# The tail of a two-layer hybrid kernel: residuals loaded during the last matrix products, one room for all late frequencies, and a last piece in halves

## The chip, the cores and the metric

One core of a Trainium2 chip runs the whole program in one launch. The metric is the device time of one execution in microseconds. The core has TensorE (PE), with its weight loads shown apart as PEld, VectorE (DVE), ScalarE (ACT), GpSimd (POOL) and SyncE (SP); a "q" behind an engine's name is its sequencer, which issues transfers and waits. The transfers run on 16 DMA engines.

## What is computed

The input x is 8 sequences of 1024 tokens with 128 channels. Layer 0 is a convolutional attention, layer 1 a two-directional state space mixer and then a spectral filter bank. The last step of the reference, cut to what matters here:

```python
t = t + mixer(_ln_t(t), ...)
t = t + _L1_ffn_ref(_ln_t(t), sigma, phi, M_u, M_phi_plus, M_phi_minus, log_weights, gumbel)
...
def _compute_spectral(u, sigma, phi, Mpp, Mpm):
    U_plus, U_minus = _stu_conv(phi, u, PADDED_SL)      # causal convolution of u with 16 filters
    s = sigma ** SIGMA_POW
    out = jnp.einsum('btkd,k,kde->bte', U_plus, s, Mpp)
    out = out + jnp.einsum('btkd,k,kde->bte', U_minus, s, Mpm)
    return out
```

The kernel does the convolution in the frequency domain. For each of 128 frequencies it builds one 128x128 matrix out of all filters, applies it to the spectra of all sequences, and transforms back. What is added to the result is the residual: t after the mixer, with the direct taps already in it.

## The kernel before, in words

All of it is in `fast_kernel`; only its last two stages matter here.

**What lies in device memory ahead of them.** `ud` holds the spectra, `xa` (8 sequences x 128 x 2 blocks x 4 x 128 channels, float32) the residuals, `yd` (128 frequencies x 2 blocks x 8 sequences x 2 x 4 x 128) takes the filtered spectra.

**The matrix stage (lines 1484 to 1586).** The 128 frequencies go in 16 chunks of 8. For chunk c+1, `matrices` (L1499) makes matrices on PE from `mst` and `taps`; ACT and DVE copy them out of PSUM into `gs` (L1510, L1512), a tile of 64 KB per partition with two buffers. For chunk c, `apply` (L1533) multiplies them with the spectra `u` (two buffers), and `gather` (L1548 to L1554, ACT and DVE) adds the parts and stores them in `yd` with one transfer of SP (L1556), twice per chunk. The two are interleaved by hand; the loop runs from c = -1 to 15, so that in its last turn (c = 15) there is only `apply`. `fetch(c)` (L1564, SP) loads what chunk c gave for block 0 and sequences 0 to 3 back as rows of `early_yt`, two transfers of 64 KB each; it waits for that chunk's stores.

**The inverse stage (lines 1588 to 1631).** There are four pieces: two blocks k, two halves h of the sequences. A piece has its frequencies `yt` (two transfers of 1 MB each, L1599; the first piece uses `early_yt`), its residuals `res` (one transfer of 1 MB, L1601, three buffers) and four sums `z` on DVE (L1607). For each r of (0, 2, 1, 3) two matmuls of 128x128 by 128x512 (L1612; in float32 each is two instructions, so that a piece has 16) go into one PSUM tile, and DVE adds the result, times the selection `keep`, to the residual (L1619). ACT then issues the store of the piece (L1622, 1 MB). `yt` has two buffers, so the frequencies of piece 4 wait until piece 2 has been read, and the residuals of piece 4 wait until the store of piece 1 has left its buffer.

**What sets the order.** PE, DVE, ACT and POOL run the matrix stage in program order (`manual_schedule`). The order of SP's transfers is chosen by the scheduler. SP's queue is strictly in order: a transfer that waits keeps all later ones of SP waiting. Transfers of SP and ACT share eight semaphores in turn.

SP's order at the end of the kernel before: store of chunk 14 (second half), fetch 14 (first), store of chunk 15 (first half), fetch 14 (second), store of chunk 15 (second half), residuals of piece 1, fetch 15 (two), frequencies of piece 2 (two), residuals of piece 2, frequencies of piece 3 (two), residuals of piece 3, frequencies of piece 4 (two), residuals of piece 4.

Of the kernel before, what the change touches and what calls it, by code (L numbers as in the profile page):

```python
# [8 lines left out]
F32 = mybir.dt.float32  # L9
AF = mybir.ActivationFunctionType  # L10
ALU = mybir.AluOpType
AX = mybir.AxisListType
PSUM = bass.MemoryType.PSUM

P = 128
B = 8
T = 1024
NT = T // P
C = 128
# [11 lines left out]
NB = 2  # L31
# [14 lines left out]
def fast_kernel(ctx: ExitStack, tc: tile.TileContext, a: dict, out: bass.AP, bad: bass.AP):  # L46
    nc = tc.nc
# [12 lines left out]
    start = ctx.enter_context(ExitStack())  # L60
    starting = start.enter_context(tc.tile_pool(name="starting", bufs=1, side="right"))

    def ctile(shape, name):
        pool = passing
        if name in LASTING:
            pool = const
        elif name in ("fwd", "m_u"):
            pool = resid
        elif name in ("wqkv", "bout", "group", "row_le", "row_ge"):
            pool = starting  # L70
        return pool.tile(shape, F32, tag=name, name=name)

    xd = dram.tile([B, T, C], F32, name="xd")
    xa = dram.tile([B, P, NB, 4, C], F32, name="xa")
# [6 lines left out]
    yd = dram.tile([NF, NB, B, 2, 4, C], F32, name="yd")  # L81
# [23 lines left out]
    for d, m in enumerate((row_le, row_ge)):  # L105
        t = ctile([P, L], f"upto{d}")
# [11 lines left out]
        out=group, in_=group, pattern=[[-4, 32], [0, 4]], compare_op=ALU.is_ge, fill=0.0, base=0, channel_multiplier=1  # L118
    )
    nc.gpsimd.affine_select(  # L120
        out=group, in_=group, pattern=[[4, 32], [0, 4]], compare_op=ALU.is_ge, fill=0.0, base=3, channel_multiplier=-1
# [76 lines left out]
    keep = ctile([P, NB], "keep")  # L198

    fwd = ctile([P, 4, 2, NF], "fwd")  # L200
    inv = ctile([P, 4, 2, P], "inv")
# [385 lines left out]
    with ExitStack() as s:  # L587
# [6 lines left out]
        p2 = s.enter_context(tc.tile_pool(name="a_2", bufs=2))  # L594
        p4 = s.enter_context(tc.tile_pool(name="a_4", bufs=4))
        ps_t = s.enter_context(tc.tile_pool(name="a_ps_t", bufs=3, space=PSUM))
        ps_o = s.enter_context(tc.tile_pool(name="a_ps_o", bufs=1, space=PSUM))
# [172 lines left out]
        for n in range(len(units) + 2):  # L770
            if n < len(units):
                prs[n] = scores(*units[n])
            if 2 <= n and units[n - 2][2] % 2:
                b, half, j = units[n - 2]
# [3 lines left out]
            if 1 <= n < len(units) + 1:  # L778
                b, half, j = units[n - 1]
# [42 lines left out]
    with ExitStack() as s:  # L822
        p1 = s.enter_context(tc.tile_pool(name="b_1", bufs=1))
        p2 = s.enter_context(tc.tile_pool(name="b_2", bufs=2))
# [16 lines left out]
        def wide_psum(pool, name):  # L841

            return pool.tile([P, 1024], F32, tag="w", name=name)
# [419 lines left out]
        for at, u in enumerate(units[:-1]):  # L1263
# [41 lines left out]
            b = (u.b + 2) % B  # L1305
# [34 lines left out]
        u = units[-1]  # L1340
# [48 lines left out]
        po = wide_psum(ps_w, "pu0").rearrange("p (k r c) -> p k r c", k=NB, r=4)  # L1389
# [22 lines left out]

    with ExitStack() as s:
        mp = s.enter_context(tc.tile_pool(name="c_m", bufs=1, side="right"))
        mst = mp.tile([P, 32, C], F32, name="mst")
        early_yt = mp.tile([P, 2, 4, 4, C], F32, name="early_yt")

        with ExitStack() as s2:
            p1 = s2.enter_context(tc.tile_pool(name="f_1", bufs=1))
            p2 = s2.enter_context(tc.tile_pool(name="f_2", bufs=2))  # L1420
            ps_f = s2.enter_context(tc.tile_pool(name="f_ps_f", bufs=2, space=PSUM))
            ps_t = s2.enter_context(tc.tile_pool(name="f_ps_t", bufs=1, space=PSUM))
            ps_o = s2.enter_context(tc.tile_pool(name="f_ps_o", bufs=2, space=PSUM))
# [60 lines left out]
        with ExitStack() as s2:  # L1484
            p2 = s2.enter_context(tc.tile_pool(name="g_2", bufs=2))
            p3 = s2.enter_context(tc.tile_pool(name="g_3", bufs=3))
            ps_g = s2.enter_context(tc.tile_pool(name="g_ps_g", bufs=8, space=PSUM))
# [3 lines left out]
            def matrices(c, n, gs):  # L1491

                nonlocal turn
                pts = [ps_g.tile([P, 4, P], F32, tag="g", name=f"pg{c}_{n}_{g}") for g in range(4)]
                cols = slice(c * FC, (c + 1) * FC)
                for e in range(4):
                    for g in range(4):
                        rows = slice(g * 32, (g + 1) * 32)
                        nc.tensor.matmul(  # L1499
                            pts[g][:, e, :],  # L1500
                            lhsT=mst[rows, n * 4 + e, :],
                            rhs=taps[rows, cols].rearrange("p f q m i -> p (f q m i)"),
                            start=True,
                            stop=True,
                        )
                for g, pt in enumerate(pts):
                    to = gs[:, :, n * 16 + g * 4 : n * 16 + g * 4 + 4]
                    frm = pt.rearrange("p e n -> p n e")
                    if turn % 2:
                        nc.vector.tensor_copy(to, frm)  # L1510
                    else:
                        nc.scalar.copy(to, frm)  # L1512
                    turn += 1

            def loaded_spectra(c):

                u = p2.tile([P, 2, NB, B, 2, 4 * FC], F32, tag="u", name=f"u{c}")
                for k in range(NB):
                    nc.sync.dma_start(
                        u[:, 0, k].rearrange("p b i f -> p b (i f)"), ud[c][:, :, k].rearrange("p b i q f -> p b (i q f)")  # L1520
                    )
                nc.gpsimd.tensor_scalar(u[:, 1, :, :, 0, :], u[:, 0, :, :, 1, :], -1.0, None, ALU.mult)  # L1522
                nc.gpsimd.tensor_copy(u[:, 1, :, :, 1, :], u[:, 0, :, :, 0, :])
                return u
# [35 lines left out]
            def fetch(c):  # L1560

                rows = slice(c * FC, (c + 1) * FC)
                for i in range(2):
                    nc.sync.dma_start(early_yt[rows, i], yd[rows, 0, 0:4, i])  # L1564

            chunks = NF // FC
            gs, us, gathered = {}, {}, {}
            s2.enter_context(tc.manual_schedule(engines=IN_ORDER))
            for c in range(-1, chunks):
                if c + 1 < chunks:  # L1570
                    gs[c + 1] = p2.tile([P, P, C], F32, tag="gs", name=f"gs{c + 1}")
                    us[c + 1] = loaded_spectra(c + 1)

                for n in range(4):
                    if c + 1 < chunks:
                        matrices(c + 1, 2 * n, gs[c + 1])
                        matrices(c + 1, 2 * n + 1, gs[c + 1])
                    if c >= 0:
                        half, turn = divmod(n, 2)
                        py = ps_g.tile([P, 2, C], F32, tag="g", name=f"py{c}_{n}")  # L1580
                        apply(c, half, turn, gs[c], us[c], py)
                        apply(c, half, turn + 2, gs[c], us[c], py)
                        gather(c, half, turn, py)
                if c > 0:
                    fetch(c - 1)
            fetch(chunks - 1)

        with ExitStack() as s2:
            p2 = s2.enter_context(tc.tile_pool(name="i_2", bufs=2))
            p3 = s2.enter_context(tc.tile_pool(name="i_3", bufs=3))  # L1590
            ps_o = s2.enter_context(tc.tile_pool(name="i_ps_o", bufs=4, space=PSUM))

            def loaded(k, h):

                yt = early_yt
                if k or h:
                    yt = p2.tile([P, 2, 4, 4, C], F32, tag="yt", name=f"yt{k}_{h}")
                    for i in range(2):
                        nc.sync.dma_start(yt[:, i], yd[:, k, h * 4 : h * 4 + 4, i])  # L1599
                res = p3.tile([P, 4, 4, C], F32, tag="res", name=f"res{k}_{h}")  # L1600
                nc.sync.dma_start(res, xa[h * 4 : h * 4 + 4, :, NB - 1 - k].rearrange("b p r c -> p b (r c)"))  # L1601
                return yt, res

            def back(k, h, yt, res):
                z = p2.tile([P, 2, 2, 4, C], F32, tag="z", name=f"z{k}_{h}")
                for r, i, op in ((0, 0, ALU.subtract), (0, 1, ALU.add), (1, 0, ALU.add), (1, 1, ALU.subtract)):
                    nc.vector.tensor_tensor(z[:, r, i], yt[:, i, :, 2, :], yt[:, 1 - i, :, 3, :], op)  # L1607
                blk = NB - 1 - k
                for r in (0, 2, 1, 3):
                    po = ps_o.tile([P, 4, C], F32, tag="o", name=f"pz{k}_{h}_{r}")  # L1610
                    for i in range(2):
                        nc.tensor.matmul(  # L1612
                            po,
                            lhsT=inv[:, r, i, :],
                            rhs=z[:, r // 2, i] if r % 2 else yt[:, i, :, r // 2, :],
                            start=(i == 0),
                            stop=(i == 1),
                        )
                    nc.vector.scalar_tensor_tensor(  # L1619
                        res[:, :, r, :], po, keep[:, blk : blk + 1], res[:, :, r, :], ALU.mult, ALU.add  # L1620
                    )
                nc.scalar.dma_start(  # L1622
                    out[h * 4 : h * 4 + 4, blk * 512 : (blk + 1) * 512].rearrange("b (p r) c -> p b (r c)", r=4), res
                )

            pieces = [(k, h) for k in range(NB) for h in range(2)]
            got = [loaded(*piece) for piece in pieces[:3]]
            for n, piece in enumerate(pieces):
                back(*piece, *got[n])
                if n + 3 < len(pieces):  # L1630
                    got.append(loaded(*pieces[n + 3]))


@with_exitstack
# [803 lines left out]
```

## Time and profile before

| what | value |
|---|---|
| time, median of 3 runs | 1452.74 us (1451.16 to 1455.33) |
| the profiled execution's own time | 1452.17 us |
| its span | 1450.4 us |
| busy over the span: PE / PEld / DVE / ACT / POOL | 92% / 58% / 77% / 63% / 36% |
| last matmul of the matrix stage ends | 1399.9 us |
| first matmul of the inverse stage starts | 1409.47 us |
| last store is issued | 1443.24 us |
| transfers `yt` / `res` / `out` of the inverse stage | 6 / 4 / 4 of 1024 KB each |

Positions are microseconds from the start of the span. In the profile's rows, "L1612 PE MATMUL pz<-yt,inv" is the matmul of line 1612 that writes `pz` from `yt` and `inv`; "idle before <-X" is how long its engine had nothing to do, and what ended that. The chain of waits follows the end of the execution back through whatever released each step.

### The profile page before, as it was taken

To read this page: it belongs to the slowest core of one execution; us is meant where nothing else is said; L and a number is where in the kernel's file an instruction comes from. 1 tells how busy PE (TensorE), PEld (TensorE's weight loads), DVE (VectorE), ACT (ScalarE), POOL (GpSimd) and SP (SyncE) were. 2 spreads that over 40 slices of the span, in tenths; PEclk is the share of its full clock that TensorE was granted. 3 is DMA by queue.
4 is the path that set the end of the run, shared out by engine and by line. 5 is a ranking of instruction groups with operands and counts; after the bars stand their busy time and mean duration, and the time that the engine had idled before them with its cause. 6 is when DMAs were issued, how large, how long until landed. Compare 5 with 4: busy or idle time off the path is not lost. (4 is left out here: it accounts for less than half of the span.)

```text
span 1450.4 us, 45285 instructions
## 1 busy us (share of the span) xinstructions
PE 1341.4 (92%) x19782; PEld 842.2 (58%) x19782; DVE 1119.2 (77%) x2138; ACT 915.4 (63%) x1421; POOL 528.1 (36%) x510
## 2 busy tenths in 40 slices
PE   5999999999998899999989999999789899999977
PEld 2223333233333566666666666666679899999963
DVE  5779889688768598989898989898554677777745
ACT  2666666666756677778777777776344455555520
POOL 3327866875500332334342323233377111111100
PEclk9999999999999999999999999999989999999989
DMA  7101111110002333434333444442368323222258
GB/s 178 41 1 30 45 38 37 37 52 23 8 1 47 82 79 75 103 75 103 89 90 89 91 93 108 96 98 48 99 200 223 97 70 91 73 76 69 72 149 320
DMA packets 139382, 123.09 MB, mean 85 GB/s; under 512 B 44808, under 2 KB 118152, under 8 KB 135080
## 3 DMA queue, kind: packets, MB, share of 16 engines
q1 hardware_dynamic: 137064, 115.93, 31.1%
q10 hardware_dynamic: 2112, 4.19, 0.8%
q8 instruction: 157, 2.57, 0.7%
q14 instruction: 49, 0.40, 0.1%
HBM read 78.15 MB, written 34.08 MB: 77 GB/s over the span
## 5 line engine op out<-in xcount | busy, mean ns | idle before, releaser
L692 ACT ACTIVATE pr<-pt 128x1024 f32<-128x1024 f32 x256 | 248.1, 1021 | 117.2 <-PE pt L687 115.7
L717 DVE TENSOR_TENSOR two<-pr,pr 128x1024 f32<-128x1024 f32 x128 | 163.4, 1317 | 21.4 <-ACT pr L692 20.5
L1512 ACT COPY gs<-pg 128x512 f32<-128x512 f32 x256 | 132.7, 602 | 64.2 <-PE pg L1499 47.8
L1510 DVE COPY gs<-pg 128x512 f32<-128x512 f32 x256 | 158.7, 682 | 15.1 <-PE pg L1499 9.7
L687 PE MATMUL pt<-q,k 32*128 32x512 f32 x1024 | 160.1, 653 | 7.0 <-ACT pr L692 4.7
L1499 PE MATMUL pg<-taps,mst 32*128 32x128 f32 x4096 | 145.9, 282 | 4.7 <-ACT gs L1512 3.8
L1499 PEld LDWEIGHTS pg<-taps,mst 32*128 32x128 f32 x4096 | 134.1, 190 | 16.7 <-issue 11.4
L922 POOL TENSOR_TENSOR ec<-ec,ct 128x2048 f32<-128x2048 f32 x16 | 83.4, 5212 | 163.9 <-ACT cums L864 143.0
L708 PE MATMUL po<-pr,v 128*32 128x512 f32 x1024 | 141.7, 609 | 0.0
L1533 PE MATMUL py<-gs,u 128*32 128x128 f32 (+1 forms) x4096 | 128.2, 277 | 0.2 <-DVE gs L1510 0.2
L964 DVE SCALAR_TENSOR_TENSOR xs<-xp,cw,xs 128x1024 f32<-128x1024 f32 x96 | 121.8, 1282 | 3.5 <-issue 1.7
L986 PE MATMUL pb<-bxt,wbc 128*128 128x512 f32 x256 | 115.7, 605 | 8.6 <-ACT zs L977 6.0
L1533 PEld LDWEIGHTS py<-gs,u 128*32 128x32 f32 (+1 forms) x4096 | 112.2, 141 | 7.7 <-DVE gs L1510 0.4
L1522 POOL TENSOR_SCALAR u<-u 128x512 f32<-128x512 f32 x16 | 23.9, 1497 | 229.2 <-PE pg L1499 157.6
L687 PEld LDWEIGHTS pt<-q,k 32*128 32x128 f32 x1024 | 47.3, 186 | 86.2 <-issue 30.3
L1085 DVE SCALAR_TENSOR_TENSOR state<-state,dec,pst 128x64 f32<-128x64 f32 x448 | 87.4, 274 | 1.1
L986 PEld LDWEIGHTS pb<-bxt,wbc 128*128 128x128 f32 x256 | 47.7, 192 | 67.1 <-issue 54.9
L1133 PE MATMUL sy<-lm,xdt 64*64 64x64 f32 x2048 | 68.3, 224 | 17.5 <-DVE state L1085 10.5
L1194 POOL TENSOR_TENSOR rms<-rms_v,mhalf 128x8 f32<-128x8 f32 x16 | 26.2, 1636 | 151.3 <-DVE rms_v L1192 151.3
L708 PEld LDWEIGHTS po<-pr,v 128*32 128x32 f32 x1024 | 27.7, 110 | 89.5 <-issue 85.3
L1133 PEld LDWEIGHTS sy<-lm,xdt 64*64 64x64 f32 x2048 | 61.3, 136 | 30.8 <-issue 28.1
L908 POOL TENSOR_TENSOR lm<-cs,lm 128x2048 f32<-128x2048 f32 x16 | 57.9, 3617 | 46.6 <-DVE xs L964 19.5
(280 smaller groups left out, 2808.3 us busy)
## 6 DMA issues: line engine op xcount, KB each, us to landing
lm<-cd SPq DMA_DIRECT2D x32, 512.0 KB
ec<-cd SPq DMA_DIRECT2D x32, 512.0 KB
ud<-sp SPq DMA_DIRECT2D x8, 1024.0 KB
u<-ud SPq DMA_DIRECT2D x32, 256.0 KB
yd<-sums SPq DMA_DIRECT2D x32, 256.0 KB
moved<-state SPq DMA_DIRECT2D x48, 128.0 KB
yt<-yd SPq DMA_DIRECT2D x6, 1024.0 KB
X<-in_x SPq DMA_DIRECT2D x8, 512.0 KB
```

Source lines behind the costliest of these rows:

```text
L687: nc.tensor.matmul(pt[:, i, :], lhsT=k[rows, j * P : (j + 1) * P], rhs=q[rows, cols], start=True, stop=True)
L692: nc.scalar.activation(pr[:, 2 * g : 2 * g + 2, :].rearrange("p i t -> p (i t)"), pt.rearrange("p i t -> p (i t)"), AF.Exp, scale=SCALE,)
L708: nc.tensor.matmul(po[rows, :], lhsT=vs[b][:, j, rows], rhs=pr[:, h, :], start=(j == 0), stop=(j == NT - 1))
L717: nc.vector.tensor_tensor(two, sums["pr"][:, 2 * g : 2 * g + 2, :], pr[:, 2 * g : 2 * g + 2, :], ALU.add)
L964: u.convolved = nc.vector.scalar_tensor_tensor(acc, xp[:, at : at + T], cw[u.d][:, n, i : i + 1], acc, ALU.mult, ALU.add)
L986: nc.tensor.matmul(u.pb[:, i * 512 : (i + 1) * 512], lhsT=wbc[u.d][:, k, :], rhs=xt[:, at : at + 512], start=(k == 0), stop=(k == KC - 1),)
L1085: nc.vector.scalar_tensor_tensor(u.state[:, k, h, :], u.state[:, k - 1, h, :], u.dec[:, c, h, j : j + 1], u.pst[c][:, j, h, :], ALU.mult, ...
L1133: nc.tensor.matmul(u.py[c][h * HP : (h + 1) * HP, r, j, :], lhsT=left, rhs=right, start=(kind == 0), stop=(kind == 1 or k is None),)
L1499: nc.tensor.matmul(pts[g][:, e, :], lhsT=mst[rows, n * 4 + e, :], rhs=taps[rows, cols].rearrange("p f q m i -> p (f q m i)"), start=True, ...
L1510: nc.vector.tensor_copy(to, frm)
L1512: nc.scalar.copy(to, frm)
L1533: nc.tensor.matmul(py[t * 32 : t * 32 + 32 - 16 * m, q // 2, :], lhsT=u[:, i, m:, :, :, q * FC + f].rearrange("p k b i -> p (k b i)"), rhs ...
```

## The change

In the last turn of the matrix loop, where no further matrices are made, the free buffer of `gs` is taken as `room` (four slots of 16 KB per partition), and the room of `mst`, which nothing reads any more, as `res1`. Three of the four megabytes of residuals are loaded there: all of block 1 in one transfer of 2 MB (`res1`), and sequences 0 to 3 of block 0 in one of 1 MB (slot 0 of `room`). They stand in SP's queue ahead of the last stores and fetches. The frequencies of pieces 2, 3 and 4 go into slots 1, 2 and 3 of `room`, so that none waits for a buffer; the last residuals (1 MB) stand between those of piece 3 and piece 4. `z` uses the two buffers of `u`, and the PSUM tiles are the eight of the matrix stage instead of four of their own. The last piece is done in two halves of two sequences: 32 matmul instructions of 256 columns for 16 of 512, eight residual adds of half the size, two stores of 0.5 MB.

SP's order at the end of the changed kernel: store of chunk 14 (first half), residuals of block 1 (2 MB), store of chunk 14 (second half), residuals of block 0 (first megabyte), store of chunk 15 (first half), fetch 14 (first), store of chunk 15 (second half), fetch 14 (second), fetch 15 (two), frequencies of piece 2 (two), of piece 3 (two), last residuals, frequencies of piece 4 (two). On PE the four matmul instructions that use `early_yt` for one r now follow one another; before, the first factors of r = 0 and r = 2 came ahead of the second ones. Ahead of this tail the instructions of every engine stand in the same order in both kernels.

```diff
-        mst = mp.tile([P, 32, C], F32, name="mst")
+        mst = mp.tile([P, 32, C], F32, tag="mst", name="mst")
...
+            def load_residuals(k, b, n):
+                nc.sync.dma_start(
+                    res[k][:, b : b + n].rearrange("p b r c -> p b (r c)"),
+                    xa[b : b + n, :, k].rearrange("b p r c -> p b (r c)"),
+                )
+
...
                 if c + 1 < chunks:
                     gs[c + 1] = p2.tile([P, P, C], F32, tag="gs", name=f"gs{c + 1}")
                     us[c + 1] = loaded_spectra(c + 1)
+                else:
+
+                    room = p2.tile([P, P, C], F32, tag="gs", name="room")
+                    res = [room[:, :32, :], mp.tile([P, 32, C], F32, tag="mst", name="res1")]
+                    res = [t.rearrange("p (b r) c -> p b r c", b=B) for t in res]
+                    load_residuals(1, 0, B)
+                    load_residuals(0, 0, 4)
...
-        with ExitStack() as s2:
-            p2 = s2.enter_context(tc.tile_pool(name="i_2", bufs=2))
-            p3 = s2.enter_context(tc.tile_pool(name="i_3", bufs=3))
-            ps_o = s2.enter_context(tc.tile_pool(name="i_ps_o", bufs=4, space=PSUM))
...
+            pieces = [(k, h) for k in range(NB) for h in range(2)]
+            yts = [early_yt]
+            for n, (k, h) in enumerate(pieces[1:], 1):
+
+                yts.append(room[:, 32 * n : 32 * n + 32].rearrange("p (i b q) c -> p i b q c", i=2, b=4))
+                for i in range(2):
+                    nc.sync.dma_start(yts[n][:, i], yd[:, k, h * 4 : h * 4 + 4, i])
+                if n == 2:
+                    load_residuals(0, 4, 4)
+            for yt, (k, h) in zip(yts, pieces):
+                z = p2.tile([P, 2, 2, 4, C], F32, tag="u", name=f"z{k}_{h}")
...
+                size = 2 if (k, h) == pieces[-1] else 4
+                for b in range(0, 4, size):
+                    bs = slice(b, b + size)
+                    to = res[blk][:, h * 4 + b : h * 4 + b + size]
+                    for r in (0, 2, 1, 3):
+                        po = ps_g.tile([P, 4, C], F32, tag="g", name=f"pz{k}_{h}_{b}_{r}")[:, :size]
+                        for i in range(2):
+                            nc.tensor.matmul(
+                                po,
+                                lhsT=inv[:, r, i, :],
+                                rhs=z[:, r // 2, i, bs] if r % 2 else yt[:, i, bs, r // 2, :],
+                                start=(i == 0),
+                                stop=(i == 1),
+                            )
+                        nc.vector.scalar_tensor_tensor(
+                            to[:, :, r, :], po, keep[:, blk : blk + 1], to[:, :, r, :], ALU.mult, ALU.add
                         )
...
+                    nc.scalar.dma_start(
+                        out[h * 4 + b : h * 4 + b + size, blk * 512 : (blk + 1) * 512].rearrange(
+                            "b (p r) c -> p b (r c)", r=4
+                        ),
+                        to.rearrange("p b r c -> p b (r c)"),
                     )
```

More of the change, by code (lines that the diff above doesn't have):

```diff
@@ L1586, in fast_kernel @@
             fetch(chunks - 1)
-        with ExitStack() as s2:
-            p2 = s2.enter_context(tc.tile_pool(name="i_2", bufs=2))
-            p3 = s2.enter_context(tc.tile_pool(name="i_3", bufs=3))
-            ps_o = s2.enter_context(tc.tile_pool(name="i_ps_o", bufs=4, space=PSUM))
[L1593 to L1605, printed above, removed]
+            pieces = [(k, h) for k in range(NB) for h in range(2)]
[8 more added lines that the diff above has]
+                z = p2.tile([P, 2, 2, 4, C], F32, tag="u", name=f"z{k}_{h}")
                 for r, i, op in ((0, 0, ALU.subtract), (0, 1, ALU.add), (1, 0, ALU.add), (1, 1, ALU.subtract)):
@@ L1608, in back @@
                 blk = NB - 1 - k
[L1609 to L1617, printed above, removed]
-                        )
-                    nc.vector.scalar_tensor_tensor(
-                        res[:, :, r, :], po, keep[:, blk : blk + 1], res[:, :, r, :], ALU.mult, ALU.add
-                    )
@@ L1622, in back @@
[L1622 to L1631, printed above, removed]
+                size = 2 if (k, h) == pieces[-1] else 4
```

## The prediction

> **What bounds the tail now.** The change touches only the end, so I read the last 60 us: first the chain of waits, then busy time by stretches, then the instructions in order of time. In the chain (start, length, what) three transfers alternate with two stretches of work:
>
> ```profile
> 1401.63 7.35 DMA res<-xa
> 1408.98 0.49 issue
> 1409.47 9.94 PE pz L1612 x16
> ...
> 1420.34 9.47 DMA out<-res
> ...
> 1429.83 10.57 DMA res<-xa
> ...
> 1440.49 2.08 DVE res L1619 x3
> ```
>
> The first transfer is the residual load of piece 1. PE doesn't need it, but the fetch of `early_yt` was issued behind it. The last residuals are issued only when the store of piece 1 has landed (1420.34 + 9.47), and DVE's last sums wait for them until 1440.49. In the table by stretches (length; busy PE, PEld, DVE, ACT, POOL with counts; clock; DMA share; GB/s) two resources are full at once:
>
> ```profile
> 1391.00:1396.00 5.00, 5.00 (x186) 5.00 (x190) 2.80 (x9) 1.48 (x4) 0.00 (x0) 1.00 0.16 56
> 1396.00:1402.00 6.00, 3.89 (x144) 3.62 (x134) 2.26 (x10) 0.80 (x3) 0.00 (x0) 1.00 0.22 71
> 1403.00:1406.00 3.00, 0.00 (x0) 0.00 (x0) 0.00 (x0) 0.00 (x0) 0.00 (x0) 0.82 0.94 301
> 1406.00:1409.00 3.00, 0.00 (x0) 0.00 (x0) 0.00 (x0) 0.00 (x0) 0.00 (x0) 0.50 1.11 154
> 1412.00:1440.00 28.00, 26.25 (x58) 11.34 (x57) 16.87 (x26) 0.00 (x0) 0.00 (x0) 0.94 1.05 398
> ```
>
> From 1412 to 1440 transfers run at 398 GB/s, their limit here, and PE works 26.25 of 28 us. From 1391 to 1402, transfers are at 16 to 22%: room to which loads can move. Taking load off the DMA queue therefore wins only what PE waits: before piece 1, before piece 4, and at the end. In order of time:
>
> ```profile
> 1401.20 0.32 SPq L1556 DMA_DIRECT2D yd<-sums  x1
> 1401.63 0.37 SPq L1601 DMA_DIRECT2D res<-xa  x1
> 1403.52 0.64 SPq L1564 DMA_DIRECT2D early_yt<-yd  x2
> ...
> 1409.47 6.49 PE L1612 MATMUL pz<-early_yt,inv 128*128 128x512 f32 x8 [9.59 <-DMA res<-xa]
> ...
> 1436.60 1.98 PE L1612 MATMUL pz<-yt,inv 128*128 128x512 f32 x4 [1.75 <-DMA yt<-yd]
> ...
> 1440.49 2.73 DVE L1619 SCALAR_TENSOR_TENSOR res<-pz,keep,res 128x512 f32<-128x512 f32 x4 [1.31 <-DMA res<-xa]
> ...
> 1443.24 0.38 ACTq L1622 DMA_DIRECT2D out<-res  x1
> ```
>
> **The change, step by step** (all against the profiled execution, 1452.17 us, of which 1450.4 are its span).
>
> 1. Start of piece 1. The last store of `yd` is issued at 1401.20 and the fetch that needs it at 1403.52, 2.32 us later; the fetch lands at 1409.2 and 1409.9 (semaphore landings in the trace) because it stands behind the residuals issued at 1401.63. The same fetch for chunk 14, issued at 1396.36 into a quiet queue, had landed by 1399.0: 2.6 us. Early bound: 1403.5 + 2.6 + 0.3 from landing to matmul = 1406.4. But at 1406 to 1409 the queue moves only 154 GB/s, just when fetch and first frequencies read what was newly written; if that belongs to these reads and not to the residuals, only the time behind the residuals goes, some 1.7 us (their packets end at 1406.2 in the trace; the fetch's own would begin about 1 us after issue): 1409.5 - 1.7 = 1407.8. I take 1407.2, and 0.2 for stores behind the moved loads (step 5): 1407.4. Gain **2.1** (bounds 3.1 and 0).
>
> 2. PE's own work stays. Piece 1 takes 9.94 us (1409.47 to 1419.41), of which some 2.8 are the clock at 0.50 until 1415. PE will still idle 7.5 us (1399.9 to 1407.4) where it idled 9.6, and the clock fell 5 us after the last matmul (it is 0.82 over 1403 to 1406): I charge the same slow start. Pieces 2 to 4 take 6.86 us each (16 instructions, 0.43 apart).
>
> 3. Wait before piece 4. Piece 3 starts at 1426.10 and piece 4 at 1432.97, and PE would end at 1440.0; it ends at 1442.0. Gain **2.0**, if the frequencies of piece 4 land in time. They are needed at 1407.4 + 9.94 + 2 x 6.86 = 1431.1. Seven loads of 1.05 MB start near 1404.8: 2.8 us at 154 GB/s move 0.43 MB, the other 6.9 take 17.4 at 398: 1425.0; the stores of piece 1 and of a part of piece 2 go between (1.05 to 1.5 MB, 2.6 to 3.8 us), and a landing takes 1 to 1.6: 1428.6 to 1430.4. Just in time: I charge **0.3** (bounds 0 and 2). No load waits for a buffer any more; what is late next is this queue itself.
>
> 4. The end. Today the last add ends 1.2 us after the last matmul (1443.2 against 1442.0), since DVE waited for residuals. With them there, one half-size add is left: between 0.28 (128x128 add, L1553) and 0.75 (L1619), 0.4 by the middle. Gain **0.75**. The last store, issued at 1443.24, is followed by 7.2 us to the span's end; its packets fill 1444.1 to 1447.1. Half of these 3.0 us is 1.5; half of 1.05 MB at 398 GB/s is 1.3: gain **1.4** between the two. The 32 instructions of 256 columns aren't new to the trace: L539 has 128x256 in 3.62 us for 16, that is 0.216 apart and 6.9 for 32. Cost 0, because the weight load (0.19) still fits beneath; were it not to, 0.19 each on top would be 6, but the row excludes that.
>
> 5. The moved loads. `res1` waits for PE's last use of `mst` (1390.9); behind it in SP's queue stand the store of chunk 14 (ready 1394.2, so SP isn't late), the third megabyte, the stores of chunk 15 and the fetches. 3.15 MB at 398 GB/s are 7.9 us, from 1392 to 1400, and the two stores between them 1.3 us. Together, 3.67 MB at 398 take 9.2, to 1401.2, just when the last store is issued: cost about 0.2. At 301 GB/s (row 1403 to 1406) they take 12.2 us, to 1404.2, where the last store's packets ended at 1402.9 before: cost 1.3; at 154 it is the slower rival below. Below 0 nothing is to be had, since the store can't be issued before DVE is done. POOL's queue isn't passed. `z` in the buffers of `u` and eight PSUM tiles add no wait: both were last read at 1399.9, and pieces are four tiles apart. Issue order of PE in piece 1 costs nothing as long as both fetches land together (0.75 us apart today, charged in step 1's range).
>
> Sum: -2.1 - 2.0 + 0.3 - 0.75 - 1.4 = **-5.95**, 1446.2 on the profiled execution. The median of the runs shown is 0.6 above it: **1446.8**.
>
> [...]
>
> [...]
>
> **Rivals.**
> - *Piece 1 doesn't start earlier* (no change). The slow 3 us after 1406 come from reading fresh rows, and the store lands later behind the loads: step 1 gives 0, piece 4's frequencies come 1.5 late. Left are 2.0 - 1.5 + 0.75 + 1.4 = 2.65: 1449.5 by the profile, **1450.1** by the median. For it: 154 GB/s beside a PE that does nothing. Against: fetch 14 took 2.6 us on rows as fresh. Chance 0.22.
> - *The loads block the stores* (slower). `res1` and the third megabyte start from an idle queue and read at the 154 GB/s of 1406 to 1409: 3.67 MB take 23.8 us, from 1392 to 1416; the last store is done 13 us later than at 1402.9, and piece 1 starts not at 1407.2 but at 1420.2, 10.7 later than today: +10.7 - 2.0 - 0.75 - 1.4 = +6.6, 1458.7 by the profile, **1459.3** by the median. It is slower by over 0.3% once piece 1 starts 8.5 us late, that is from 20.8 us for the 3.67 MB, a mean below 176 GB/s. A delayed instruction fetch of PE behind these loads would add to it. For it: the row at 154. Against: that stretch lasts 3 us, and 28 us follow at 398. Chance 0.10.
> - *Frequencies get the whole queue and the clock rises sooner* (more gain): start at 1406.4, 1.4 us less of slow clock, nothing late: 5.95 + 1.0 + 1.4 + 0.3 = 8.65, **1444.1**. Chance 0.15, inside faster.
>
> **How the numbers follow.** A difference of 0.3% (4.4 us) is about what a measurement can tell from no change. The forecast has 0.53 and the better case 0.15: faster 0.68. Same 0.22, slower 0.10. The range reaches from the better case with 1 us more, 1443.0, over the no-change rival with 0.9 more, 1451.0.
>
> **What would show it.** Right: first matmul of the inverse stage at 1406.5 to 1408; no wait of PE ahead of piece 4; last store issued near 1438.7; transfers at over 300 GB/s in 1392 to 1401. Wrong: a first matmul after 1409.5 with the last `yd` store landing after 1405; PE idle between pieces on `yt`; `apply` of chunk 15 ending after 1400.5.

## The result, and the profile after

The changed kernel takes **1450.45 us** (median of 8 runs, 1447.21 to 1453.01), the kernel before in the same runs 1453.97 us (8 runs, 1449.04 to 1456.55): ratio **0.9975**, 95% interval 0.9958 to 0.9992. So it is faster, by about 3.5 us, not by the 5.95 us of the sum. By the prediction's own mark of 0.3% that size still counts as "no change", though the interval leaves out 1. Two repetitions below gave 0.9962 and 0.9973.

The profiled execution took 1450.32 us, its span 1448.4. To compare tails I count from **M**, the end of the last matrix matmul (L1499), because everything ahead of it is the same work: M is 1390.94 before and 1391.83 after, 0.9 apart in work that the change doesn't touch. Counted from M:

| us after M | before | after | difference |
|---|---|---|---|
| last `apply` matmul ends | 8.94 | 10.89 | **+1.95** |
| last store of `yd` issued | 10.26 | 12.19 | +1.93 |
| fetch 15 issued | 12.58 | 14.62 | +2.04 |
| first inverse matmul starts | 18.53 | 18.30 | -0.23 |
| last inverse matmul ends | 51.07 | 49.58 | -1.49 |
| last add ends | 52.27 | 50.11 | -2.16 |
| end of the span | 59.50 | 56.55 | **-2.95** |

The fetch does wait less (from its issue to the first matmul 3.67 us for 5.95), but everything ahead of it ends two microseconds later. The chain of waits of the changed kernel (start, length, what) shows why:

```profile
1391.83 8.27 PE py L1533 x231
1400.10 1.49 issue
1401.59 1.15 PE py L1533 x27
...
1404.02 2.42 DMA yd<-sums
...
1406.45 3.32 DMA early_yt<-yd
...
1410.12 31.30 PE pz L1624 x80
```

Two things are new. From 1410.12 to 1441.43 PE runs without a wait: the waits for `yt` and for the residuals are gone. And 1.49 us have appeared inside `apply`, which is nothing but matmuls whose data have long been there; "issue" means that the profile shows nothing that PE waited for. In order of time (start, length, engine, line, operation, count, idle time before it) the stop stands 28 matmuls before the end, and SP has two residual loads out by then:

```profile
1391.76 8.34 PE L1533 MATMUL py<-gs,u 128*32 128x128 f32 x292
1391.86 0.39 SPq L1567 DMA_DIRECT2D res<-xa  x1
...
1395.54 0.37 SPq L1567 DMA_DIRECT2D room<-xa  x1
...
1401.59 1.13 PE L1533 MATMUL py<-gs,u 128*32 128x128 f32 x28 [1.49 <-issue]
```

The kernel before does all 320 of these matmuls in one go:

```profile
1390.88 9.01 PE L1533 MATMUL py<-gs,u 128*32 128x128 f32 x320
```

What PE lacked were its own instructions, as experiments 1 to 4 show. Queue q8, of kind "instruction", brings them in packets of 16 KB (157 packets, 2.57 MB over the span of the kernel before, for PE's 39564 matmuls and weight loads: 252 a packet), and the profile counts these on the same 16 DMA engines. In the kernel before, the DMA view of 1395.9 to 1396.2 shows one such packet and no other queue (packets, MB, share of 16 engines); it starts 5.08 us after M:

```profile
q8 instruction: 1, 0.02, 19.4%
```

The same place in the changed kernel, counted from M, is 1396.9. There, over 1395.9 to 1399.2, the queue of the loads (q1) has all engines full and no instruction packet starts:

```profile
DMA packets 616, 1.24 MB, mean 375 GB/s; under 512 B 11, under 2 KB 11, under 8 KB 616
...
q1 hardware_dynamic: 616, 1.24, 103.3%
```

It comes in the next stretch, 1399.2 to 1399.5, 7.47 us after M, 2.4 us late:

```profile
q1 hardware_dynamic: 60, 0.11, 99.1%
q8 instruction: 1, 0.02, 19.7%
```

PE goes on 2.3 us after that packet starts. The table by stretches (length; busy PE, PEld, DVE, ACT, POOL; clock; DMA share; GB/s) answers to the one of before:

```profile
1391.80:1400.10 8.30, 8.30 (x293) 8.06 (x292) 4.26 (x15) 2.10 (x7) 0.00 (x0) 1.00 0.89 303
1400.00:1403.00 3.00, 1.23 (x30) 0.86 (x28) 0.00 (x0) 0.20 (x1) 0.00 (x0) 1.00 1.03 394
1406.00:1409.00 3.00, 0.00 (x0) 0.00 (x0) 0.00 (x0) 0.00 (x0) 0.00 (x0) 0.50 0.42 74
1411.00:1430.00 19.00, 19.00 (x40) 8.11 (x39) 12.69 (x20) 0.00 (x0) 0.00 (x0) 0.86 1.05 392
```

The empty room of 1391 to 1402 is filled as intended. From 1411 to 1430 PE is never idle (26.25 of 28 us before). The row of 1406 to 1409 can't be set beside the one of before (74 GB/s for 154), since fetch 15 is issued at 1406.45 here and at 1403.52 there. What can be compared are the 2 us in which the fetch and the first frequencies are read from `yd`, in the DMA view (packets, MB, share of 16 engines), 1407 to 1409 before and 1408 to 1410 after:

```profile
q1 hardware_dynamic: 92, 0.17, 105.2%
```

```profile
q1 hardware_dynamic: 128, 0.25, 94.7%
```

By share and count a packet takes some 0.37 us before and 0.24 after, where the loads of 1395.9 to 1399.2 take 0.09 a packet. These reads are slow in both kernels, and no residual load stands among them now.

### The profile page after: what moved, and what is told of

Its sections match the earlier page's. It is cut to its first block, busy times and chain, and to the rows that moved or that the text cites. A ratio compares the mean times of both kernels' runs of the same rounds, so it can differ in the third digit from the quotient of the medians.

```text
span 1448.4 us, 45312 instructions
## 1 busy us (share of the span) xinstructions
PE 1341.9 (93%) x19798; PEld 846.2 (58%) x19798; DVE 1118.5 (77%) x2142; ACT 915.1 (63%) x1421; POOL 528.0 (36%) x510
## 3 DMA queue, kind: packets, MB, share of 16 engines
q8 instruction: 157, 2.57, 0.8%
## 5 line engine op out<-in xcount | busy, mean ns | idle before, releaser
L1510 DVE COPY gs<-pg 128x512 f32<-128x512 f32 x256 | 158.7, 682 | 14.4 <-PE pg L1499 9.7
L1499 PE MATMUL pg<-taps,mst 32*128 32x128 f32 x4096 | 146.0, 281 | 4.0 <-ACT gs L1512 3.1
L1499 PEld LDWEIGHTS pg<-taps,mst 32*128 32x128 f32 x4096 | 134.0, 189 | 16.1 <-issue 11.5
```

Source lines behind the costliest of these rows:

```text
L1499: nc.tensor.matmul(pts[g][:, e, :], lhsT=mst[rows, n * 4 + e, :], rhs=taps[rows, cols].rearrange("p f q m i -> p (f q m i)"), start=True, ...
```

## The experiments

**Theory A**: the 2 MB load delays PE's instruction packet, PE stops, and that eats the gain of the earlier fetch. **Rival B**: the loads' writes or their use of memory slow `apply` itself, whatever the instruction packets do. **Rival C** (the first rival of the prediction): the fetch is slow because it reads fresh rows. All positions are counted from M of the same run.

**1. The loads alone, on the kernel before.** `idle` is read by nothing.

```diff
-        mst = mp.tile([P, 32, C], F32, name="mst")
+        mst = mp.tile([P, 32, C], F32, tag="mst", name="mst")
...
+                else:
+                    idle = mp.tile([P, 32, C], F32, tag="mst", name="idle")
+                    nc.sync.dma_start(
+                        idle.rearrange("p (b r) c -> p b (r c)", b=B), xa[:, :, 1].rearrange("b p r c -> p b (r c)")
+                    )
```

> The kernel before with one more transfer: 2 MB of residuals into the room of mst, at the place of the changed kernel's first moved load; nothing reads them, all else stays. Theory (instruction fetch of PE behind the load): a gap of PE of about 1.5 us, 8.3 us after the last matrix matmul, and the first matmul of the inverse stage about 2 us later than before (20.4 for 18.5). Rival (the gap is a dependency of the changed kernel): no gap, 18.5 as before.

Measured: 1454.39 us in one run. The direction is A's, the size is not: PE stopped once, for 2.90 us, 3.5 us sooner than expected, and `apply` ended at 15.21, 6.27 later than before. Its matmul groups, and PE's waits of 1380 to 1404 (us in total, times, longest):

```profile
1386.61 4.84 PE L1533 MATMUL py<-gs,u 128*32 128x128 f32 x164
1394.36 7.53 PE L1533 MATMUL py<-gs,u 128*32 128x128 f32 x156 [2.90 <-issue]
```

```profile
PE py L1533 <- issue: 2.9, 1, 2.9
```

The stop accounts for about half of the 6.27 us. The rest is PE's clock, which fell during the stop (table by stretches, ahead of the stop, with it, and behind it):

```profile
1386.70:1391.20 4.50, 4.50 (x164) 4.50 (x164) 2.79 (x9) 1.53 (x5) 0.00 (x0) 1.00 0.76 238
1391.20:1394.30 3.10, 0.25 (x8) 0.01 (x1) 0.06 (x1) 0.00 (x0) 0.00 (x0) 0.89 1.03 377
1396.00:1398.00 2.00, 2.00 (x44) 1.85 (x40) 0.89 (x4) 0.27 (x1) 0.00 (x0) 0.50 0.01 2
```

At a clock of 1.00 PE does 164 of these matmuls in 4.5 us, at 0.50 only 44 in 2 us.

The packet due at 1.0 (it starts 1.02 us after M in the kernel before) was served only at 5.09; the next ones at 8.79 and 14.4. In the changed kernel the packet due at 1.0 was served at 1.06, although the load there is issued at the same place (0.03 after M): it started at 1392.88, and the first packet of the load 0.04 us later, at 1392.92. So the first packet and the load's first packets run a race, and a lost one brings a stop 128 matmuls sooner: here a long one that cost the clock too, in experiments 2 and 8 the first of two.

**2. The same bytes without writing on-chip memory.** The load is a copy from device memory to device memory. A 64 KB store of `half`, put ahead, only sets its start.

```diff
+                if (c, n, turn) == (chunks - 2, 1, 0):
+                    nc.sync.dma_start(idle[:, 0, :C], half)
+                    nc.sync.dma_start(idle, xa[:, :, 1].rearrange("b p r c -> p b (r c)"))
...
+            idle = dram.tile([P, B, 4 * C], F32, name="idle")
```

> The kernel before with a copy of 2 MB inside device memory (plus 64 KB ahead of it to set its moment), at about the same moment; nothing reads it. It touches no on-chip memory but that first 64 KB. Theory (DMA engines busy, instruction fetch waits): PE stops for 1 to 4 us between 4 and 10 us after the last matrix matmul, with no packet of the instruction queue inside the copy. Rival (writing into on-chip memory slows PE's reads): no gap.

Measured: 1454.63 us in one run. Instruction packets at 3.85 and 8.44; PE stops after the same 164 and 292 matmuls:

```profile
1389.66 4.84 PE L1533 MATMUL py<-gs,u 128*32 128x128 f32 x164
1396.07 3.76 PE L1533 MATMUL py<-gs,u 128*32 128x128 f32 x128 [1.57 <-issue]
1400.37 1.13 PE L1533 MATMUL py<-gs,u 128*32 128x128 f32 x28 [0.54 <-issue]
```

`apply` ends at 11.77. Writes to on-chip memory are not needed for the stop, which takes that half of B away; the other half, memory reads, falls with the next run.

**3. The changed kernel with its instructions moved.** 32 matmuls near the beginning are done twice (the same result), so that packet boundaries move by 128 instructions, 64 matmuls with their weight loads; the loads stay.

```diff
-                for e in range(4):
+                for e in list(range(4)) * (2 if c == 0 and n < 2 else 1):
```

> The changed kernel with 32 matmuls of the very first matrices made twice (same result): 128 more PE instructions, 1200 us back into the stage's start, which moves the boundaries of 16 KB in PE's instruction stream about 2 us earlier against the program. Theory (the fetch that falls into the load waits until the load ends): the gap starts at about 6.4 instead of 8.3 us after the last matrix matmul and ends at the same 9.7, so it lasts about 3.4 us instead of 1.5; apply ends near 12.8 instead of 10.9. Rival (anything that depends on the place in the program or on the load alone): gap of 1.5 at 8.3, as in the changed kernel.

Measured: 1450.53 us in one run. The stop moved with the instructions, from after 292 matmuls to after 228, exactly 64 earlier:

```profile
1391.54 6.59 PE L1533 MATMUL py<-gs,u 128*32 128x128 f32 x228
1400.76 2.88 PE L1533 MATMUL py<-gs,u 128*32 128x128 f32 x92 [2.63 <-issue]
```

`apply` ended at 12.03. The stop was shorter than the 3.4 us expected, but its place is what B can't give: the traffic is the same, and the place of the stop follows the count of instructions.

**4. The moved loads put back into the tail**, one ahead of each piece's frequencies, all else as changed.

```diff
-                    load_residuals(1, 0, B)
-                    load_residuals(0, 0, 4)
...
             fetch(chunks - 1)
+            load_residuals(1, 0, 4)
...
-                if n == 2:
-                    load_residuals(0, 4, 4)
+                load_residuals(*((1, 4, 4), (0, 0, 4), (0, 4, 4))[n - 1])
```

> The changed kernel with its three moved megabytes of residuals back in the tail (piece 1's right behind the fetches of chunk 15, the others each behind the frequencies of the piece before); room, halves and eight PSUM tiles kept. Positions count from the end of the last matrix matmul (L1499). Theory (the loads keep PE's instruction fetch waiting): PE's apply of chunk 15 has no gap and ends at 9.0, as before, where the changed kernel has 10.9; the first matmul of the inverse stage comes at 15.6 to 16.6 (before 18.5, changed 18.3). Rival (the gap comes from the new buffers or from the order on PE): the gap of 1.5 us stays. On both the queue is the bound of the rest: PE waits 3 to 5 us for the frequencies of piece 4 and the residuals behind them end it within 1.5 us of the kernel before. Second question: if the fetch of early_yt lands within 2.9 us of its issue with a residual load behind it, slow reads come from the frequencies that follow it; if it needs over 3.3, from the fetch itself.

Measured: 1459.07 us in one run (1447.98 for one of before); M came 4.0 us later than in the changed kernel. `apply` ends at 8.93, without a stop, and the first inverse matmul starts at 15.73, 3.45 after its fetch was issued. So a residual load *behind* the fetch doesn't hold it up, and C falls as it was priced: piece 1 starts 3.45 us after the fetch's issue, against 5.95 before, although the rows are as fresh. A part of C stays. The fetch lands 3.36 us after its issue (3.32 in the changed kernel, by its chain), just over the mark of 3.3 that the expectation set for a fetch that is slow itself; chunk 14's took 2.6 us in the kernel before. Whether the age of the rows makes these reads slow, or their form (one fetch goes into 8 of the 128 partitions of `early_yt`), no run separates.

The 3 MB, however, now stand in the queue that the pieces wait for:

```profile
1430.78 2.84 PE L1624 MATMUL pz<-room,inv 128*128 128x512 f32 x6 [2.09 <-DMA room<-yd]
...
1439.50 0.70 PE L1624 MATMUL pz<-room,inv 128*128 128x256 f32 x2 [2.45 <-DMA room<-yd]
1442.27 2.93 PE L1624 MATMUL pz<-room,inv 128*128 128x256 f32 x6 [2.07 <-DMA room<-yd]
```

PE waits 6.6 us in three places, more than the 3 to 5 expected. The span ends at 61.35, 4.8 later than in the changed kernel and 1.85 later than before (at most 1.5 was expected). Moving the loads is right, in spite of the stop: 2.57 us of later start buy 8.42 us of a shorter inverse stage (1.05 of them are lost again between PE's last matmul and the end of the span).

**5. The last piece whole**, all else as changed.

```diff
-                size = 2 if (k, h) == pieces[-1] else 4
+                size = 4
```

> The changed kernel with its last piece whole again (16 matmuls of 512 columns, four adds, one store of 1 MB); all else stays. Positions from the last matrix matmul, or from the first matmul of the inverse stage where the start wanders. Forecast's view: the halves are worth 1.4 us behind the last add and 0.35 in the last add itself, and cost nothing on PE: from first matmul to span's end 38.3 + 1.7 = 40.0. Rival (halves give less, since the last piece's matmuls wait for z, 7.6 us instead of 6.9, and two stores queue behind each other): 38.3 + 0.5 = 38.8.

Measured: 1452.06 us in one run. From first matmul to the end of the span it takes 38.60 us, for 38.25 in the changed kernel, but that sum can't judge the halves: piece 1, which they don't touch, took 9.29 us here and 9.99 there, because the clock rose 4.7 us after its first matmul here and 6.1 there. From the first matmul of the last piece to the end of the span it is 15.58 us whole and 14.53 in halves (14.55 with the moved instructions, 14.20 and 14.57 in the repetitions). So halves win 1.0 to 1.4 us here, of which 0.36 is a wait of the whole piece for its frequencies; forecast were 1.7, by the rival 0.5. Behind the last matmul they save 1.23 us (8.19 for 6.96). They cost something on PE that the prediction set at nothing. In the changed kernel's last piece (order of time, the first half):

```profile
1433.85 1.89 PE L1624 MATMUL pz<-room,inv 128*128 128x256 f32 x8
...
1434.72 2.49 DVE L1614 TENSOR_TENSOR z<-room 128x512 f32<-128x512 f32 x4
...
1435.57 2.38 PE L1624 MATMUL pz<-z,inv 128*128 128x256 f32 x8
1436.06 0.30 PEld L1624 LDWEIGHTS pz<-z,inv 128*128 128x128 f32 x2 [0.29 <-DVE z L1614]
```

The matmuls that don't need `z` last 1.89 us in a half and 3.60 in a whole piece that waits for nothing; DVE first finishes the add of piece 3 and then needs 2.49 for `z`, so PE catches up with it.

**6. The loads spread.** One megabyte of block 1 is loaded at chunk 8 into a tile of its own, `early_res`; the other goes where the 2 MB went; the third waits until two quarters of chunk 15 are done. SP follows program order in the last turn.

```diff
+        early_res = mp.tile([P, 4, 4, C], F32, name="early_res")
...
-                    load_residuals(1, 0, B)
-                    load_residuals(0, 0, 4)
+                    load_residuals(1, 4, 4)
+                if c == 8:
+                    nc.sync.dma_start(
+                        early_res.rearrange("p b r c -> p b (r c)"), xa[0:4, :, 1].rearrange("b p r c -> p b (r c)")
+                    )
...
+                        if (c, n) == (chunks - 1, 1):
+                            load_residuals(0, 0, 4)
```

> The changed kernel with the moved loads spread: the residuals of piece 1 (1 MB) far earlier, in chunk 8, into 8 KB per partition of their own; those of piece 2 (1 MB) at the place of the 2 MB load, into mst's room; those of piece 3 (1 MB) behind the first store of chunk 15. SP's last transfers stand in program order. Theory: a load of 1 MB is through 4.6 us after the last matrix matmul, ahead of the fetch due at 5.1: no gap (if the fetch due at 1.0 isn't caught), apply ends at 9.0, first inverse matmul at 16.7 (changed: 18.3), span's end at 55 (changed 56.5, before 59.5): ratio to before 0.9965 to 0.997. Rival (bytes, not the length of one burst, slow PE): the gap stays over 1 us, end at 56.5, ratio 0.9975.

Measured (5 rounds): 1452.89 us, ratio 0.9985 (0.9969 to 1.0001). In the tail A holds: the packet due at 5.1 is served at 5.94, and PE stops for only 0.2 us (too short for the groups in order of time, which show 320 matmuls in one go); `apply` ends at 9.38.

```profile
1397.04 9.45 PE L1534 MATMUL py<-gs,u 128*32 128x128 f32 x320
```

But the third megabyte now stands before the last store: fetch 15 goes out at 15.05, piece 1 starts at 18.58, and PE waits 1.8 us before the last piece. The span ends at 56.22, 0.3 better than the changed kernel, where 55 was expected. In this execution (1455.21 us, above the median) M is at 1397.11, 5.3 us later than in the changed kernel; 4.6 of these are there already when the matrices of chunk 1 begin (1151.2 for 1146.6), ahead of the load in chunk 8. One trace can't say whether the worse median comes from there too.

**7. The same with the two tiles exchanged**, so that the third megabyte goes to the room of `mst` and the second to that of `gs`.

```diff
-                    res = [room[:, :32, :], mp.tile([P, 32, C], F32, tag="mst", name="res1")]
+                    res = [mp.tile([P, 32, C], F32, tag="mst", name="res0"), room[:, :32, :]]
```

> As e7, but the residuals of piece 2 go into the free buffer of gs, which is read until about 2.0 us after the last matrix matmul, so the load starts 2 us later and can't catch the fetch due at 1.0; those of piece 3 and 4 go into mst's room. Theory: the fetch due at 5.1 meets the last microsecond of that load and is late by up to 1.5 us, which PE's lead over its fetch (about 1.1) nearly hides: gap of 0 to 0.4, apply ends at 9.0 to 9.4, span's end at 55 to 55.5, and never the double stop of e2: ratio 0.9965 to 0.997, with less spread than e6. Rival: as for e7.

Measured (5 rounds): 1453.72 us, ratio 0.9982 (0.9962 to 1.0002); packet at 7.51, a stop of 1.4 us, `apply` to 10.83, a wait of 1.0 before the last piece, end at 56.36, M 1395.76. The expectation, a stop of at most 0.4 and an end by 55.5, missed: the packet due at 5.1 waited 2.4 us although the load ahead of it was half as large.

**8. Two bursts of a megabyte.** `early_res` as in 6; 1 MB right after the last matrices, the third behind the second store of chunk 14.

```diff
-                    load_residuals(1, 0, B)
                     load_residuals(0, 0, 4)
...
+                    if (c, n) == (chunks - 2, 3):
+                        res = [None, mp.tile([P, 32, C], F32, tag="mst", name="res1")]
+                        res[1] = res[1].rearrange("p (b r) c -> p b r c", b=B)
+                        load_residuals(1, 4, 4)
```

> As e7 (residuals of piece 1 in chunk 8, those of piece 2 at the place of the 2 MB load), but the residuals of piece 3 go behind the second store of chunk 14, so that their packets are gone before the last store, which they delayed in e7; SP in program order from chunk 14 on. Theory (a fetch waits for packets that already stand ahead of it, here at most one burst of 1 MB): the fetch due at 5.1 is served between 5.5 and 8, gap of PE 0 to 1.5 us, apply ends at 9.0 to 10.4; the last store is not held back (3.7 us from apply's end to the fetch of chunk 15, where e7 had 5.7), first inverse matmul at 16.6 to 17.8, span's end at 54.5 to 56 after the last matrix matmul (changed 56.6 and 56.8, e7 56.2). Rival (what the gap loses less the queue takes at piece 4): end at 56 or more, with a wait of over 1.5 us ahead of piece 4.

Measured (5 rounds): 1453.58 us, ratio 0.9986 (0.9965 to 1.0007). The profiled execution lost the race of experiment 1 with half the bytes: packets at 3.48 (due at 1.0) and 8.88, and two stops, again after 164 and 292 matmuls:

```profile
1393.12 4.83 PE L1534 MATMUL py<-gs,u 128*32 128x128 f32 x164
1399.20 3.75 PE L1534 MATMUL py<-gs,u 128*32 128x128 f32 x128 [1.26 <-issue]
1404.32 1.13 PE L1534 MATMUL py<-gs,u 128*32 128x128 f32 x28 [1.36 <-issue]
```

`apply` ends at 12.27 (10.4 at most was expected), the span at 57.34 (56). The rival's wait ahead of piece 4 isn't there either: PE has none in the inverse stage.

**9. The changed kernel again**, beside 5 to 7 and beside 8.

> The changed kernel once more, on the chip of the two that follow. Theory: the fetch due 1.0 us after the last matrix matmul races with the first packets of the 2 MB load (1.1). Where the fetch wins, as in the profile, PE stops once, for 1.5 us; where it loses, as with the idle load of e2, twice, for 6. So its times spread, and its mean gain over before is 1 to 4 us: ratio 0.997 to 1.000. Rival: the gap is always 1.5, ratio 0.9975 as measured.

> The changed kernel on the chip of e9, for a comparison of the two: one gap of 1.5 to 2.3 us in apply, the fetch of instructions served 7.5 to 8.1 us after the last matrix matmul, span's end at 56.5 to 57, ratio to before 0.996 to 0.9985. If e9 is better by its tail alone, it shows 1 to 2 us (0.1%) below this, about as much as the spread of the medians.

Measured (5 rounds each): 1450.35 us, ratio 0.9962 (0.9948 to 0.9977), and 1450.97 us, ratio 0.9973 (0.9951 to 0.9995). One stop in either profile, of 2.0 and 1.9 us, and the first packet at 1.07 and 0.90: none of the three profiles of the changed kernel lost the race. The "twice, for 6" of the first expectation took the 6 us of experiment 1 for two stops. None of the versions 6 to 8 beat it: their medians are higher, though the intervals overlap.

Taken together, the runs give the size of a stop. In those without moved instructions, PE reaches the matmul after the packet boundary 4.5 or 8.0 us after M when nothing held it before, and goes on 2.2 to 2.6 us after the packet's start. For the boundary at 8.0:

| run | packet starts | PE goes on | stop (start less 8.0) |
|---|---|---|---|
| loads spread (6) | 5.94 | 8.26 | 0.3 |
| changed | 7.47 | 9.76 | 1.8 |
| tiles exchanged (7) | 7.51 | 9.70 | 1.7 |
| changed, third time | 7.79 | 10.19 | 2.2 |
| last piece whole (5) | 7.85 | 10.30 | 2.3 |
| changed, again | 8.08 | 10.30 | 2.3 |

So the stop is the packet's start plus 2.3 less 8.0, and the packet of 5.1 may come about 0.6 us late at no cost. (The stops are the gap between the starts of two matmuls; the idle time that the trace gives is about 0.3 less, one matmul.) The clock can add to it. In the repetition beside 5 to 7 it falls after the stop:

```profile
1402.00:1402.70 0.70, 0.70 (x12) 0.20 (x4) 0.00 (x0) 0.00 (x0) 0.00 (x0) 0.50 0.44 149
```

There `apply` ends 1.6 us after PE goes on, in experiment 5 1.9, for 1.1 in the changed kernel.

## Why the prediction was right and wrong

It was right in sign, and the waits that it meant to shorten did get shorter; but the largest term, the earlier start, was nearly all eaten by a cost that the sum left out. The time lies inside the range near its slow end, 3.65 above the forecast. Counted from M, 3.0 of the 5.95 us are missing. Two of the prediction's own three signs of being wrong came true: `apply` ends at 1402.72 (after 1400.5), and the first matmul comes at 1410.12 (after 1409.5) with the last store of `yd` landing at 1406.44 (after 1405). M is 0.9 later here than in the profile of before; without that the matmul would come at 1409.2, but `apply` would still end at 1401.8. That the time is in the range all the same is partly luck. The slow end was set by the rival without a gain at the start, and a stop that this rival doesn't contain brought the total to within 0.4 of its 1450.1; a lost race as in experiments 1, 2 and 8 would have cost 1 to 4 us more. Step by step:

- **Step 5 is the one that failed.** "Cost about 0.2" counted only what stands behind the moved loads in SP's queue: the stores. That term was right: from the end of `apply` to the last store's issue 1.30 us for 1.32, and to fetch 15's issue 3.73 for 3.64. Instruction packets of PE, which go through the same engines from another queue, were mentioned only as an addition in a rival with 0.10, without a price. They cost **1.95**; that the stop comes from them is shown by experiments 1 to 4.
- **Step 1**: the fetch-to-matmul part was 3.67 us, as the prediction had it (3.7, from 1403.5 to 1407.2), a gain of 2.28. Gain of the start after step 5's loss: 0.23 for 2.1. The rival "piece 1 doesn't start earlier" has about the right total for the wrong reason: the store wasn't late behind the loads, it was issued late because `apply` ended late. Its doubt about the reads of fresh rows was half right: they are slow without the residuals too, but they took the fetch 3.3 us to its landing, not the 5.7 of before.
- **Step 2**: the clock stays low as charged (0.50 in the row from 1406). The idle time was 7.4 us for the 7.5 assumed. The clock rose 6.1 us after the first matmul where it had risen after 5.7, so piece 1 takes 9.99 us for 9.76 (to the first matmul of piece 2). Pieces 2 and 3 take 6.87 each, as the row had it.
- **Step 3**: the wait before piece 4 went, 2.0 us, and the 0.3 charged for the queue wasn't paid. It had little left: in experiment 6 the last frequencies are issued at 23.87 after M for 23.52 and needed 1.0 us sooner, since piece 1 is shorter, and PE waits 1.8 us.
- **Step 4**: the last add ends 0.52 us after the last matmul for 1.20, a gain of 0.68 for 0.75. The half-size store gains **0.79** for 1.4: 6.44 us from the last add to the end of the span, for 7.23. Most of its packets are out between 1442.5 and 1444.5, but single ones go on to 1446 and beyond. And "cost 0" of the halves was wrong: from its first matmul to the end of its last one the last piece takes 7.56 us, for 7.03 in pieces 2 and 3, since halves shorten the cover of `z`. The working excluded weight loads as a cost and didn't ask for DVE's `z`.

Sum from M: -0.23 at the start; on PE -2.01 for the wait, +0.53 for the halves and +0.23 for the clock in piece 1; -0.68 and -0.79 behind it: -2.95.

One sum in the slower rival is off, without effect here: a start 8.5 us late, reckoned back as its own 10.7 was, needs 21.7 us for the 3.67 MB, a mean of 169 GB/s, not 20.8 and 176.

What stays open: why M comes 4 to 5 us later than in the changed kernel in the profiles of experiments 4, 6 and 7 (1395.8 to 1397.1, for 1386.7 to 1393.2 in all others). Most of it (3.4 to 4.6 us) is there when the matrices of chunk 1 begin, ahead of every load that these edits move or add. Executions of one kernel differ by as much (the changed kernel's eight by 5.8 us), so it may be no more than that; a tail is judged here from M, not by the total of one execution. And how often the changed kernel loses the race for the first packet: three profiles can't tell.

## What to carry to other kernels

Before moving a large load into a stretch where the DMA engines look idle, look up the instruction queue in the DMA view: if an engine is running short instructions there without pause, a burst of loads can delay its instruction packets (by 0.9 to 4.1 us here), and what looked like free room can cost a stop on the critical engine (1.49 us in the changed kernel, 2.90 in experiment 1). Price it as the packet's start plus the time from there to the engine's next instruction (2.2 to 2.6 us here), less the time at which the engine needs it; a packet that was only 0.9 us late cost little (0.2 us, experiment 6), and a stop in which the clock fell cost more (3.1 us more in experiment 1). And when a last piece is cut for a shorter tail, check each thing that was hidden beneath the whole piece (here DVE's 2.49 us for `z`), not only the engine that is cut.

## What the runs showed of the hardware

- An instruction packet of 16 KB served 128 of these matmuls with their weight loads: stops came after 164 matmuls (experiments 1, 2 and 8) and after 292 (the changed kernel, experiments 2, 7 and 8), 128 apart, whatever the load, and after 228, 64 earlier, when 64 were put ahead (experiment 3). In `apply` the packets start 4.06 and 3.52 us apart in the kernel before.
- Behind a load of 1 to 2 MB a packet waited 2.4 to 4.1 us in the changed kernel and in experiments 1, 7 and 8. In experiment 6 it was 0.9: there the load of 1 MB was issued 5.1 us before the packet was due, in experiment 7, with a wait of 2.4 us, 3.1 before. An estimate from the 0.09 us that a packet of the loads takes over 1395.9 to 1399.2: 2.4 to 4.1 us are the time of some 27 to 46 such packets on one engine. In what order an engine takes the packets of two queues, no run shows.
- PE's clock fell in some of these stops and not in others. After 2.90 us without work (experiment 1) it was 0.50 over 1396 to 1398, and after a stop of 2.0 us in a repetition of the changed kernel 0.50 over 1402 to 1402.7. After 1.49 us in the changed kernel it was 1.00 over 1400 to 1403, and after 2.63 us (experiment 3) PE did the last 92 matmuls in 2.88 us, about the pace of experiment 8, where 128 took 3.75 us and the clock was 1.00 over 1400 to 1403.
- The first moved load, from an idle queue, started slowly although its rows are old. The 2 MB of residuals were issued at 1391.86; the DMA view of 1391 to 1402 in 40 slices of 0.275 us reaches over 330 GB/s 2.4 us after that:

```profile
GB/s 0 0 0 0 30 0 67 112 37 209 253 313 335 424 402 410 402 417 417 380 424 395 387 365 194 357 387 410 380 425 439 365 402 365 402 395 395 432 395 424
```
